# A graph layer on one core: the loop taken in sets of two units, seeds under three parts, and the sixth block of comparisons moved to VectorE

## The chip, the cores and the metric

The kernel runs on one core of a Trainium2 chip. The metric is the device time of one execution in microseconds. Five engines work at once, each through its own queue in order: TensorE (PE; its weight loads are shown as PEld), VectorE (DVE), ScalarE (ACT), GpSimd (POOL) and SyncE (SP), which here only issues DMAs. They wait for each other by semaphores.

## The reference

One layer of a graph network: 6250 nodes of 64 values, 206250 edges sorted by target node.

```python
h = jnp.maximum(_layernorm(x, axis=-1), 0.0)
msg = jax.nn.relu(h[src] + edge_attr)
agg = jax.ops.segment_sum(msg, dst, num_segments=x.shape[0])
out = x + (jax.nn.relu((h + agg) @ W1 + b1) @ W2 + b2)
```

## The kernel before, in words

**Groups and units.** The edges are taken in 269 groups of 768: 128 partitions of G = 6 columns, 64 values each. For most groups the source rows of the first three columns are fetched by GpSimd with three indirect DMAs from a table in DRAM (`gather`, L198, one per column, 128 rows each); the rows of the last three columns (H = 3) are made on the chip by TensorE. Three such columns are a *unit*. In 12 groups (`WHOLE`, L64) all six columns are made on the chip: two units and no gather. After five groups of a prologue, which are gathered entirely, 276 units follow, and two units are a *set*: 138 sets.

**How TensorE fetches rows.** `hp` holds all node rows as three bf16 parts (high, middle, low: 3 x 64 columns), by node. `find` (L446, VectorE) compares the list of wanted nodes with each partition's own number: 0/1 weights `found`. `slots_of` (L478) multiplies them with `hp` and collects the wanted rows into slots; one call makes two of the twelve blocks of a set, here called a *pair of slots*, in a PSUM bank `half` of three. `slots_out` (L486, ScalarE) casts a pair to bf16, `picked`. `back` (L465, VectorE) compares places with `ids` and gives the 0/1 weights `backs` that bring slots back to the edges' order, for five of the six blocks of a set; the sixth is made by two activations on ScalarE (`back_far` L455: a distance; `back_near` L458: relu of one less the distance). `pick` (L493) multiplies `backs` with `picked`, 18 matmuls a unit, into a PSUM buffer `pick` of two banks, of which there are two. It holds four rows of 4 x 64 values: three columns of the unit with their three parts, with the edge attributes as a fourth part (`room`, L499, ScalarE), and in the fourth row the window sums.

**What follows.** `messages` adds the gathered rows to the attributes (L560), reduces the four parts to one sum (L563, VectorE, 768 elements in) and takes the relu (L565, ScalarE). `one_hot` (L544) compares each edge's target with 32 window places; `window_sum` (L575, TensorE) sums the group's messages by target; `sum_into_z` (L538, VectorE) adds the window into `z` at a place held in a register. Every so often a block of 512 nodes is complete, and `hidden`, `result` and `store` write it out. The `rank_*` functions and `source` prepare the lists for three sets at a time, in steps spread over six units (`chunk`); some are matmuls (L277, L315, L329) that wait for VectorE's step before.

**The order.** Scheduling is by hand: each engine works in the order in which the Python code issues. `half(u)` is one unit's turn: window sum of the unit before, three pairs of slots for the set ahead, products of the next unit, z addition of two units before, messages, one-hot, then half of the comparisons. Gathers are issued AHEAD = 9 groups early; their buffers (LOOK = 12) are freed by L560.

Of the kernel before, what the change touches and what calls it, by code (L numbers as in the profile page):

```python
# [81 lines left out]
def kernel(  # L82
# [239 lines left out]
    def source(c):  # L322
# [38 lines left out]
    def ln_turn(r, m, h):  # L361
        zv = z[:D, :NP].rearrange("d (p r) -> d p r", r=RR)
        for i in range(0, m, 4):
            n = min(4, m - i)
            pt = psum.tile([D, 4, PP], F32, name="half", bufs=3)
# [14 lines left out]
    def combine(xg, ea, n):  # L380
        nc.vector.tensor_tensor(xg[:, :n], xg[:, :n], ea[:, :n], ALU.add)
        msg = work.tile([P, G, D], F32, name="msg", bufs=3)
        nc.scalar.activation(msg[:, :n], xg[:, :n], AF.Relu)
        return msg
# [63 lines left out]

    far = const.tile([P, 1], F32, name="far")
    nc.vector.tensor_scalar_mul(far, ids[:, Q - 1:], -1.0)  # L450
    dists = {}

    def back_far(k):
        dists[k] = rank.tile([P, 2 * H * P], BF16, name="dist", bufs=1)
        nc.scalar.activation(dists[k], spots[k].bitcast(I16), AF.Abs, bias=far)  # L455

    def back_near(k):
        nc.scalar.activation(backs[k][:, Q - 1].rearrange("p t s -> p (t s)"), dists.pop(k), AF.Relu,  # L458
                             bias=ones[:, 0:1], scale=-1.0)

    def back(k, q0, q1):
        if q0 == 0:
            backs[k] = hot.tile([P, Q, 2 * H, P], BF16, name="backs")
        for q in range(q0, min(q1, Q - 1)):
            nc.vector.tensor_scalar(backs[k][:, q].rearrange("p t s -> p (t s)"), spots[k].bitcast(I16),  # L465
                                    ids[:, q:q + 1], None, op0=ALU.is_equal)
        if q1 == Q:
            spots.pop(k)

    def slots_of(k, n0):  # L470
        ps = psum.tile([P, 2, 3 * D], F32, name="half", bufs=3)
        for u in range(2):
# [15 lines left out]
    def pick(u0, cols):  # L488
        k, i = divmod(u0, 2)
        ps = picks[u0]  # L490
        for u in cols:
            for q in range(Q):
                nc.tensor.matmul(ps[:, u, :3].rearrange("p t d -> p (t d)"), backs[k][:, q, i * H + u, :],  # L493
                                 picked[k][:, i * Q + q], start=(q == 0), stop=(q == Q - 1))

    def room(u):
        g, c0 = UNITS[u]
        picks[u] = pick_banks[u % 2]
        nc.scalar.copy(picks[u][:, :H, 3], taken[g][0][:, c0:c0 + H])  # L499

# [16 lines left out]
    def norm_edges(xg):  # L517
# [3 lines left out]
        nc.vector.tensor_tensor(xg, xg, s.unsqueeze(2).to_broadcast([P, G, D]), ALU.subtract)  # L521
        sq = work.tile([P, G, D], F32, name="msg", bufs=3)
        nc.scalar.activation(sq, xg, AF.Square)
# [8 lines left out]

    aggs, hots, taken, msgs = {}, {}, {}, {}
    pick_banks = [psum.tile([P, H + 1, 4, D], F32, name=f"pick{i}", bufs=1) for i in range(2)]

    def sum_into_z(u):
# [3 lines left out]
    def one_hot(u):  # L540
        g, (lo, hi) = group_of(u), span(u)
        n = hi - lo
        oh = work.tile([P, G, W], F32, name="oh")
        nc.vector.tensor_tensor(  # L544
# [7 lines left out]

    def messages(u):
        g, (lo, hi) = group_of(u), span(u)
        ea, xg = taken[g]
        m = pool_cols(g)
        if g < RAW:
            norm_edges(xg)
        if m:
            nc.vector.tensor_tensor(ea[:, lo:m], ea[:, lo:m], xg[:, lo:m], ALU.add)  # L560
        if u >= 0:
            c0 = UNITS[u][1]
            nc.vector.tensor_reduce(ea[:, c0:c0 + H], picks.pop(u)[:, :H].rearrange("p j t d -> p j d t"), AX.X, ALU.add)  # L563
        msg = work.tile([P, G, D], F32, name="msg", bufs=3)
        nc.scalar.activation(msg[:, lo:hi], ea[:, lo:hi], AF.Relu)  # L565
        msgs[u] = msg
        if is_last(u):
            taken.pop(g)

    def window_sum(u):  # L570
# [46 lines left out]

    def blocks_behind(u):
        g = group_of(u)
        for c in sorted(res):  # L620
# [3 lines left out]
        for c in range(NB):  # L624
            if READY[c] == g and is_last(u):
                hid[c] = hidden(c)
# [8 lines left out]

    def half(u):
        g = group_of(u)
        k, i = divmod(u, 2)
        first = ((0, 2), (6, 8))[i]
        later = ((4,), (10,))[i]  # L640
        now = is_set(k + 1)
        if is_first(u):
            enter(g + AHEAD)
        if i == 0:
            if is_set(k + 3):
                source_load(k + 3)
        elif is_set(k + 3):
            spot_load(k + 3)
        window_sum(u - 1)
        if u + 1 < U:  # L650
            room(u + 1)
        if now:
            for n0 in first:
                slots_of(k + 1, n0)
                slots_out(k + 1, n0)
            for n0 in later:
                slots_of(k + 1, n0)
        if u + 1 < U:
            pick(u + 1, range(H))
        sum_into_z(u - LAG)  # L660
        blocks_behind(u - LAG)
        messages(u)
        if now:
            for n0 in later:
                slots_out(k + 1, n0)
        one_hot(u)
        if i == 0:
            if is_set(k + 1):
                back_near(k + 1)
                back(k + 1, 3, Q)  # L670
            if is_set(k + 2):
                find(k + 2, 0)
                find(k + 2, BB)
        else:
            if is_set(k + 2):
                back_far(k + 2)
                back(k + 2, 0, 3)
                find(k + 2, 1)
        chunk(u + 14, rank_at)
        chunk(u + 13, rank_count)  # L680
        chunk(u + 12, rank_of)
        chunk(u + 11, rank_marks)
        chunk(u + 11, rank_turn)
        chunk(u + 10, rank_holds)
        chunk(u + 10, rank_fits)
        chunk(u + 9, source)
        if g in CHECKS and is_first(u):
            find_left(CHECKS.index(g))

# [55 lines left out]
    for k in (0, 1):  # L745
        source_load(k)
        spot_load(k)
    for g in range(F0):
        enter(g + AHEAD)
        messages(g - F0)  # L750
        one_hot(g - F0)
# [11 lines left out]
        if g == 3:  # L763
            rank_at(2)
            rank_count(2)
        if g >= 1:
            window_sum(g - 1 - F0)
# [7 lines left out]

    for b in range(BB + 1):
        find(0, b)
    back_far(0)
    back(0, 0, Q)
    back_near(0)  # L780
    for n0 in range(0, 2 * Q, 2):
        slots_of(0, n0)
        slots_out(0, n0)
    source_load(2)
    spot_load(2)
    room(0)
    pick(0, range(H))
    for b in range(BB + 1):
        find(1, b)
    back_far(1)  # L790
    back(1, 0, 3)
    for u in range(U):
        half(u)
    xbs[NB] = old_rows(NB)
    for c in sorted(hid):
        res[c] = result(c, *hid.pop(c))
    window_sum(U - 1)
    for c in sorted(res):
# [19 lines left out]
    with tc.If(any_left > 0):  # L818
        nc.gpsimd.iota(wide, pattern=[[1, WB]], base=1, channel_multiplier=0, allow_small_or_imprecise_dtypes=True)
        with tc.For_i(0, NG, 1) as i:  # L820
# [3 lines left out]
            nc.vector.tensor_copy(lf, left[:, ds(i * G, G)])  # L824
            ea = edge.tile([P, G, D], F32, name="ea")
            nc.sync.dma_start(out=ea.rearrange("p j d -> p (j d)"),
# [3 lines left out]
            all_windows(combine(xa, ea, G), lf, G)  # L830
        ea = edge.tile([P, G, D], F32, name="ea")
        attr_load(ea, NG)
# [45 lines left out]
```

## Time and profile before

| | us |
|---|---|
| runs before (median of 3) | 1771.63 (1760.12 to 1772.58) |
| profiled execution, its own time | 1747.93 |
| its span, first to last instruction | 1746.2 |
| mean granted TensorE clock in it | 0.907 |

Times in the profile are microseconds unless marked ns; a name such as L478 is a line of the kernel. In lists of groups a row has the line, engine, operation, output and input, shapes and count, then busy time, the mean of one in ns, and the engine's idle time just before with what ended it. In a timeline a row has the start, the duration and the instruction, and in brackets the idle time before and its releaser. A matmul's end is modelled, and a busy PE is not PE at its peak. A table by windows gives each engine's busy time in a stretch, with its instructions in parentheses, and the granted clock (PEclk, 1.00 is full).

### The profile page before, as it was taken

Reading aid. Unit: us, or ns where it says so; the run is one execution under the profiler, and the core shown is the slowest. Engines: PE = TensorE matmul, PEld = TensorE weight load, DVE = VectorE, ACT = ScalarE, POOL = GpSimd, SP = SyncE. Lnnn points to the kernel's source line nnn. Section 1 sums busy time; section 2 is a strip of 40 time slices with the busy share of each in tenths; the row PEclk is TensorE's granted clock in tenths of the full one; section 3 lists DMA queues with packets and bytes.
Section 4 is the critical chain, followed back from the end, with each engine's and each line's share of the span. In section 5 each row is a group of like instructions: output and inputs, shape, how many; then the busy total and the mean of one; then the engine's idle time right before and its main releaser. Section 6 shows DMA issues by size and latency. Waiting matters only on the chain.

```text
span 1746.2 us, 54838 instructions
## 1 busy us (share of the span) xinstructions
PE 1302.7 (75%) x23181; PEld 991.3 (57%) x23181; DVE 1024.7 (59%) x2686; ACT 871.5 (50%) x1955; POOL 802.7 (46%) x798
## 2 busy tenths in 40 slices
PE   3047787778778778777777877877777877777787
PEld 2035566556557556565655655655665655565566
DVE  7346556546565665555755655654566566465576
ACT  4235455446455555554544544644554555454465
POOL 6734435444453553544544444444444445444430
PEclk9998889889897898989988988987899889898898
DMA  6223334334333442443433333333333334333341
GB/s 181 66 57 108 103 93 109 91 88 114 99 98 95 114 109 82 108 106 93 117 96 91 106 99 95 104 98 90 94 103 106 93 106 110 86 103 95 97 111 33
DMA packets 115095, 172.34 MB, mean 99 GB/s; under 512 B 28443, under 2 KB 83612, under 8 KB 114844
## 3 DMA queue, kind: packets, MB, share of 16 engines
q1 hardware_dynamic: 89752, 143.03, 27.4%
q0 software_dynamic: 25088, 25.74, 8.3%
q8 instruction: 184, 3.01, 0.7%
q14 instruction: 67, 0.55, 0.1%
q10 hardware_dynamic: 4, 0.01, 0.0%
HBM read 164.85 MB, written 3.84 MB: 97 GB/s over the span
## 4 chain that ended last, share of the span: by engine, by line
PE 64%; issue 18%; another core or an unknown queue 7%; ACT 6%; DVE 3%; POOL 1%; DMA 1%; DVEq 0%; ACTq 0%; POOLq 0%
PE pick L493 28%; PE half L478 24%; PE pick L575 8%; ACT picked L486 2%; PE rows L329 1%; ACT msg L565 1%; PE rows L592 1%; PE rows L603 1%; ACT dist L455 1%; PE rows L279 1%; POOL xg L198 1%; PE rows L277 1%; PE rows L315 0%; ACT backs L458 0%
## 5 line engine op out<-in xcount | busy, mean ns | idle before, releaser
L198 POOL DMA_INDIRECT xg<-h_rows,src_sb x754 | 768.0, 1019 | 865.4 <-DVE ea L560 688.2
L478 PE MATMUL half<-hp,found 128*32 128x192 bf16 x14352 | 500.8, 260 | 215.3 <-issue 191.8
L486 ACT CAST picked<-half 128x384 bf16<-128x384 f32 x828 | 381.1, 477 | 521.7 <-remote 321.7
L493 PE MATMUL pick<-picked,backs 128*128 128x192 bf16 x4968 | 574.6, 267 | 83.9 <-issue 64.2
L493 PEld LDWEIGHTS <-backs 128*128 128x128 bf16 x4968 | 446.6, 106 | 198.1 <-issue 179.6
L478 PEld LDWEIGHTS <-found 128*32 128x32 bf16 x14352 | 340.7, 100 | 320.7 <-issue 284.0
L538 DVE TENSOR_TENSOR z<-z,pick 128x32 f32 x281 | 53.1, 189 | 656.7 <-issue 236.4
L563 DVE TENSOR_REDUCE ea<-pick 128x192 f32<-128x768 f32 x276 | 262.5, 951 | 0.0
L465 DVE TENSOR_SCALAR backs<-spots,ids 128x768 bf16<-128x768 int16 x690 | 251.0, 415 | 0.0
L575 PE MATMUL pick<-oh,msg 128*64 128x32 f32 x3224 | 177.3, 237 | 54.6 <-ACT msg L565 29.5
L446 DVE TENSOR_SCALAR found<-sources,nodes_of 128x1536 bf16<-128x1536 int16 (+1 forms) x414 | 212.4, 542 | 0.1
L575 PEld LDWEIGHTS pick<-oh,msg 128*64 128x64 f32 x3224 | 138.4, 149 | 119.7 <-issue 53.7
L565 ACT ACTIVATE msg<-ea 128x384 f32<-128x384 f32 (+2 forms) x281 | 144.4, 514 | 24.5 <-DVE ea L563 12.8
L499 ACT COPY pick<-ea 128x192 f32<-128x192 f32 x276 | 88.6, 321 | 126.0 <-remote 69.4
L458 ACT ACTIVATE backs<-dist,ones 128x768 bf16<-128x768 bf16 x138 | 130.5, 946 | 0.3 <-ACT dist L455 0.3
L455 ACT ACTIVATE dist<-spots,far 128x768 bf16<-128x768 int16 x138 | 129.9, 941 | 0.0
L544 DVE TENSOR_TENSOR oh<-slot,slots 128x192 f32<-128x192 int16 (+2 forms) x281 | 95.7, 341 | 24.2 <-remote 24.2
L560 DVE TENSOR_TENSOR ea<-ea,xg 128x192 f32<-128x192 f32 x252 | 90.2, 358 | 3.4 <-issue 1.9
L277 PE MATMUL rows<-at,upper 128*128 128x432 f16 x46 | 17.0, 369 | 44.9 <-remote 24.1
L281 ACT CAST before<-rows 128x432 f16<-128x432 f32 x46 | 23.6, 514 | 48.4 <-remote 38.8
L332 ACT CAST source<-rows 24x64 int16<-24x64 f32 x138 | 27.6, 200 | 35.9 <-remote 27.6
L329 PE MATMUL rows<-holds,marks 128*96 128x96 f16 x276 | 27.6, 235 | 15.2 <-DVE oh L544 4.9
(102 smaller groups left out, 435.1 us busy)
## 6 DMA issues: line engine op xcount, KB each, us to landing
sources<-source_row SPq DMA_DIRECT2D x138, 384.0 KB
ea<-in_edge_attr_dram SPq DMA_DIRECT2D x268, 192.0 KB
spots<-spot_rows SPq DMA_DIRECT2D x138, 192.0 KB
xg<-h_rows,src_sb POOLq DMA_INDIRECT x754
xb<-in_x_dram SPq DMA_DIRECT2D x12, 128.0 KB
out_dram<-o SPq DMA_DIRECT2D x12, 128.0 KB
h_rows<-x SPq DMA_DIRECT2D x3, 384.0 KB
dst_sb<-in_dst_main_dram SPq DMA_DIRECT2D x1, 804.0 KB
```

What stands on the lines that cost most here:

```text
L198: nc.gpsimd.indirect_dma_start(out=xg[:, j, :], out_offset=None, in_=rows[:, :], in_offset=bass.IndirectOffsetOnAxis(ap=idx[:, j:j + 1], a ...
L446: nc.vector.tensor_scalar(found[k][:, b * PARTS:b * PARTS + n].rearrange("p m i s -> p (m i s)"), sources[k][:, :n * 2 * S], nodes_of[:, b ...
L455: nc.scalar.activation(dists[k], spots[k].bitcast(I16), AF.Abs, bias=far)
L458: nc.scalar.activation(backs[k][:, Q - 1].rearrange("p t s -> p (t s)"), dists.pop(k), AF.Relu, bias=ones[:, 0:1], scale=-1.0)
L465: nc.vector.tensor_scalar(backs[k][:, q].rearrange("p t s -> p (t s)"), spots[k].bitcast(I16), ids[:, q:q + 1], None, op0=ALU.is_equal)
L478: nc.tensor.matmul(ps[j * S:(j + 1) * S, u], found[k][:, m, i, :], hp[:, min(m, RR - 1)].rearrange("p t d -> p (t d)"), start=(b == 0), st ...
L486: nc.scalar.copy(picked[k][:, n0:n0 + 2], halves.pop((k, n0)))
L493: nc.tensor.matmul(ps[:, u, :3].rearrange("p t d -> p (t d)"), backs[k][:, q, i * H + u, :], picked[k][:, i * Q + q], start=(q == 0), stop ...
L544: nc.vector.tensor_tensor(oh[:, lo:hi], slot[:, g * G + lo:g * G + hi].unsqueeze(2).to_broadcast([P, n, W]), slots.unsqueeze(1).to_broadca ...
L563: nc.vector.tensor_reduce(ea[:, c0:c0 + H], picks.pop(u)[:, :H].rearrange("p j t d -> p j d t"), AX.X, ALU.add)
L565: nc.scalar.activation(msg[:, lo:hi], ea[:, lo:hi], AF.Relu)
L575: nc.tensor.matmul(pa[i * D:(i + 1) * D], msg[:, j, :], oh[:, j, :], start=(j < lo + 2), stop=(j >= hi - 2))
```

## The change

- The loop's turn is a set, `both(k)`, in place of a unit, `half(u)`. Within it the order is: window sums of the two units before; for each of the two units the reduction and addition (`total`), the seeds of the unit two ahead (`room`) and three pairs of slots with their casts; both relus; the products of both units ahead; both z additions; the one-hots; all six blocks of comparisons and three finds for the set two ahead; then the ranking steps of both units.
- `room` seeds the three parts themselves: the attributes under the high part and zeros under the other two. The products are added on top (no `start`), so the reduction takes three parts (576 elements). For one copy to do it, the attribute tiles are twelve buffers of 12 columns, the last six zero, set by ScalarE in the prologue (`tails_begin`); `banks_begin` runs a matmul over each bank of `pick` once.
- In `total` the reduction comes ahead of the addition of gathered rows.
- All six blocks of comparisons are VectorE's; `back_far` and `back_near` are gone.
- The window sums move from the `pick` buffers into the last 128 columns of the three `half` banks, which become named tiles used in turn (`next_half`).
- `msg` and `oh` get four buffers.

```diff
+    eas = [const.tile([P, 2 * G, D], F32, name=f"ea{i}") for i in range(LOOK)]
...
-        ea = edge.tile([P, G, D], F32, name="ea")
-        attr_load(ea, g)
+        ea = eas[g % LOOK]
+        attr_load(ea[:, :G], g)
...
+    half_banks = [psum.tile([P, 512], F32, name=f"half{i}", bufs=1) for i in range(3)]
+    halves_made = [0]
+
+    def next_half():
+        halves_made[0] += 1
+        return half_banks[halves_made[0] % 3]
...
-        for q in range(q0, min(q1, Q - 1)):
+        for q in range(q0, q1):
...
     def slots_of(k, n0):
-        ps = psum.tile([P, 2, 3 * D], F32, name="half", bufs=3)
+        ps = next_half()[:, :2 * 3 * D].rearrange("p (u d) -> p u d", u=2)
...
-                                 picked[k][:, i * Q + q], start=(q == 0), stop=(q == Q - 1))
+                                 picked[k][:, i * Q + q], start=False, stop=(q == Q - 1), skip_group_check=True)
...
-        nc.scalar.copy(picks[u][:, :H, 3], taken[g][0][:, c0:c0 + H])
+        parts = taken[g][0][:, H:].rearrange("p (t c) d -> p c t d", c=H)
+        if c0:
+            nc.scalar.copy(picks[u][:, :H, :3], parts)
+        else:
+            nc.scalar.copy(picks[u][:, :H, 0], taken[g][0][:, :H])
+            nc.scalar.copy(picks[u][:, :H, 1:3], parts[:, :, 1:])
...
+    def banks_begin():
+
+        for t in pick_banks:
+            flat = t.rearrange("p j t d -> p (j t d)")
+            for b in range(0, (H + 1) * 4 * D, 512):
+                nc.tensor.matmul(flat[:, b:b + 512], ones_b, mark_rows[0].rearrange("p g s j -> p (g s j)")[:, :512],
+                                 start=True, stop=True)
+
+    def tails_begin(i):
+        nc.scalar.copy(eas[i][:, G:].rearrange("p j d -> p (j d)"), zero.to_broadcast([P, G * D]))
...
-    def messages(u):
+    def total(u):
         g, (lo, hi) = group_of(u), span(u)
         ea, xg = taken[g]
         m = pool_cols(g)
+        if u >= 0:
+            c0 = UNITS[u][1]
+            nc.vector.tensor_reduce(ea[:, c0:c0 + H], picks.pop(u)[:, :H, :3].rearrange("p j t d -> p j d t"), AX.X, ALU.add)
         if m:
             nc.vector.tensor_tensor(ea[:, lo:m], ea[:, lo:m], xg[:, lo:m], ALU.add)
...
-        pa = pick_banks[u % 2][:, H].rearrange("p t d -> p (t d)")[:, u // 2 % AB * W:][:, :W]
+        pa = half_banks[u % 3][:, 2 * 3 * D + u // 3 % AB * W:][:, :W]
...
+    def both(k):
+        us = (2 * k, 2 * k + 1)
+        ahead = is_set(k + 1)
+        for u in us:
+            if is_first(u):
+                enter(group_of(u) + AHEAD)
+        if is_set(k + 3):
+            source_load(k + 3)
             spot_load(k + 3)
...
+        for u in us:
+            window_sum(u - 2)
+        for u in us:
+            total(u)
+            if ahead:
+                room(u + 2)
+                for n0 in range(u % 2 * Q, u % 2 * Q + Q, 2):
+                    slots_of(k + 1, n0)
+                    slots_out(k + 1, n0)
+        for u in us:
+            relu(u)
+        if ahead:
+            for u in us:
+                pick(u + 2, range(H))
+        for u in us:
+            sum_into_z(u - 2)
+        blocks_behind([u - 2 for u in us])
+        for u in us:
+            one_hot(u)
+        if is_set(k + 2):
+            backs_of(k + 2)
+            for b in range(BB + 1):
+                find(k + 2, b)
+        for u in us:
+            chunk(u + 14, rank_at)
...
+            if group_of(u) in CHECKS and is_first(u):
+                find_left(CHECKS.index(group_of(u)))
```

More of the change, by code (lines that the diff above doesn't have):

```diff
@@ L364, in ln_turn @@
             n = min(4, m - i)
-            pt = psum.tile([D, 4, PP], F32, name="half", bufs=3)
+            pt = next_half()[:D].rearrange("d (u p) -> d u p", u=4)
             for u in range(n):
@@ L381, in combine @@
         nc.vector.tensor_tensor(xg[:, :n], xg[:, :n], ea[:, :n], ALU.add)
-        msg = work.tile([P, G, D], F32, name="msg", bufs=3)
+        msg = work.tile([P, G, D], F32, name="msg", bufs=4)
         nc.scalar.activation(msg[:, :n], xg[:, :n], AF.Relu)
@@ L447, in find @@
                                 sources[k][:, :n * 2 * S], nodes_of[:, b:b + 1], None, op0=ALU.is_equal)
[L449 to L459, printed above, removed]
     def back(k, q0, q1):
@@ L521, in norm_edges @@
         nc.vector.tensor_tensor(xg, xg, s.unsqueeze(2).to_broadcast([P, G, D]), ALU.subtract)
-        sq = work.tile([P, G, D], F32, name="msg", bufs=3)
+        sq = work.tile([P, G, D], F32, name="msg", bufs=4)
         nc.scalar.activation(sq, xg, AF.Square)
@@ L542, in one_hot @@
         n = hi - lo
-        oh = work.tile([P, G, W], F32, name="oh")
+        oh = work.tile([P, G, W], F32, name="oh", bufs=4)
         nc.vector.tensor_tensor(
@@ L556, in messages, with relu @@
         m = pool_cols(g)
-        if g < RAW:
-            norm_edges(xg)
+        if u >= 0:
+            c0 = UNITS[u][1]
+            nc.vector.tensor_reduce(ea[:, c0:c0 + H], picks.pop(u)[:, :H, :3].rearrange("p j t d -> p j d t"), AX.X, ALU.add)
         if m:
             nc.vector.tensor_tensor(ea[:, lo:m], ea[:, lo:m], xg[:, lo:m], ALU.add)
[L561 to L566, printed above, removed]
+        totals[u] = ea
         if is_last(u):
             taken.pop(g)
+    def relu(u):
+        lo, hi = span(u)
+        msg = work.tile([P, G, D], F32, name="msg", bufs=4)
+        nc.scalar.activation(msg[:, lo:hi], totals.pop(u)[:, lo:hi], AF.Relu)
+        msgs[u] = msg
     def window_sum(u):
         (lo, hi), oh, msg = span(u), hots.pop(u), msgs.pop(u)
-        pa = pick_banks[u % 2][:, H].rearrange("p t d -> p (t d)")[:, u // 2 % AB * W:][:, :W]
+        pa = half_banks[u % 3][:, 2 * 3 * D + u // 3 % AB * W:][:, :W]
         for j in range(lo, hi):
@@ L624, in blocks_behind @@
         for c in range(NB):
-            if READY[c] == g and is_last(u):
+            if READY[c] in [group_of(u) for u in us if is_last(u)]:
                 hid[c] = hidden(c)
@@ L634, in is_set @@
         return 0 <= k < KS
[L636 to L647, printed above, removed]
-            spot_load(k + 3)
[L649 to L688, printed above, removed]
@@ new lines, in both @@
+    def both(k):
[6 more added lines that the diff above has]
+            source_load(k + 3)
+            spot_load(k + 3)
+        for u in us:
[23 more added lines that the diff above has]
+            chunk(u + 14, rank_at)
+            chunk(u + 13, rank_count)
+            chunk(u + 12, rank_of)
+            chunk(u + 11, rank_marks)
+            chunk(u + 11, rank_turn)
+            chunk(u + 10, rank_holds)
+            chunk(u + 10, rank_fits)
+            chunk(u + 9, source)
+            if group_of(u) in CHECKS and is_first(u):
+                find_left(CHECKS.index(group_of(u)))
@@ L747 @@
         spot_load(k)
+    banks_begin()
     for g in range(F0):
+        for i in range(g * LOOK // F0, (g + 1) * LOOK // F0):
+            tails_begin(i)
         enter(g + AHEAD)
-        messages(g - F0)
+        if g < RAW:
+            norm_edges(taken[g][1])
+        total(g - F0)
+        relu(g - F0)
         one_hot(g - F0)
@@ L774 @@
     hot = ctx.enter_context(tc.tile_pool(name="hot", bufs=2))
[L776 to L793, printed above, removed]
+    for k in (0, 1):
+        for b in range(BB + 1):
+            find(k, b)
+        backs_of(k)
+        if k == 0:
+            for n0 in range(0, 2 * Q, 2):
+                slots_of(0, n0)
+                slots_out(0, n0)
+            source_load(2)
+            spot_load(2)
+            for u in (0, 1):
+                room(u)
+                pick(u, range(H))
+    for k in range(KS):
+        both(k)
     xbs[NB] = old_rows(NB)
@@ L796 @@
         res[c] = result(c, *hid.pop(c))
+    window_sum(U - 2)
     window_sum(U - 1)
@@ L824 @@
             nc.vector.tensor_copy(lf, left[:, ds(i * G, G)])
-            ea = edge.tile([P, G, D], F32, name="ea")
+            ea = eas[0][:, :G]
             nc.sync.dma_start(out=ea.rearrange("p j d -> p (j d)"),
@@ L830 @@
             all_windows(combine(xa, ea, G), lf, G)
-        ea = edge.tile([P, G, D], F32, name="ea")
+        ea = eas[0][:, :G]
         attr_load(ea, NG)
```

9 lines of the change are left out of this document (5 added, 4 removed).

## The prediction

> **What bounds the kernel now.** I read the busy shares and the chain that ended last, then the waits, and then the instructions in order of time for units with and without gathers.
>
> ```profile
> span 1746.2 us, 54838 instructions
> PE 1302.7 (75%) x23181; PEld 991.3 (57%) x23181; DVE 1024.7 (59%) x2686; ACT 871.5 (50%) x1955; POOL 802.7 (46%) x798
> PE 64%; issue 18%; another core or an unknown queue 7%; ACT 6%; DVE 3%; POOL 1%; DMA 1%; DVEq 0%; ACTq 0%; POOLq 0%
> ...
> POOL xg L198 <- DVE ea L560: 688.2, 220, 19.4
> ACT picked L486 <- remote: 321.7, 147, 6.2
> DVE z L538 <- PE pick L493: 108.9, 33, 7.2
> ```
>
> The chain is TensorE and "issue", a wait for nothing that the profile shows. The wait list says when GpSimd runs: it stands 688.2 us waiting for L560, the addition that frees a gather buffer, so each unit's three gathers start right behind that addition. And ScalarE's cast L486 waits 321.7 us for a releaser that the profile cannot name. Two stretches show what these have to do with each other: one unit with gathers (487.4 on), and one set of two units whose group has none.
>
> ```profile
> core 0: us, PE busy (x) PEld busy (x) DVE busy (x) ACT busy (x) POOL busy (x), PEclk, DMA share, GB/s
> 487.40:492.80 5.40, 3.98 (x86) 3.27 (x82) 3.67 (x11) 2.94 (x8) 2.98 (x3) 1.00 0.54 137
> 682.70:689.60 6.90, 6.84 (x161) 5.92 (x163) 6.39 (x17) 6.56 (x15) 0.00 (x0) 1.00 0.50 176
> ```
>
> At the same clock of 1.00, one unit with gathers takes 5.40 us, and two without take 6.90. The rows say how; first the unit with gathers, then the one without:
>
> ```profile
> 487.43 1.26 PE L478 MATMUL half<-hp,found 128*32 128x192 bf16 x52
> 487.51 0.36 DVE L560 TENSOR_TENSOR ea<-ea,xg 128x192 f32<-128x192 f32 x1
> 488.14 0.94 POOL L198 DMA_INDIRECT xg<-h_rows,src_sb  x1 [1.63 <-DVE ea L560]
> 488.75 0.46 ACT L486 CAST picked<-half 128x384 bf16<-128x384 f32 x1
> 489.39 1.09 POOL L198 DMA_INDIRECT xg<-h_rows,src_sb  x1 [0.30 <-issue]
> 490.26 0.48 ACT L486 CAST picked<-half 128x384 bf16<-128x384 f32 x1 [1.05 <-remote]
> 490.78 0.94 POOL L198 DMA_INDIRECT xg<-h_rows,src_sb  x1 [0.30 <-issue]
> 492.58 0.48 ACT L486 CAST picked<-half 128x384 bf16<-128x384 f32 x1 [1.42 <-remote]
> ...
> 686.43 1.26 PE L478 MATMUL half<-hp,found 128*32 128x192 bf16 x52
> 687.08 0.86 ACT L486 CAST picked<-half 128x384 bf16<-128x384 f32 x2
> ```
>
> The 52 matmuls make three pairs of slots (20, 16, 16). Both times they are through in 1.26 us. Without gathers the first two casts follow at once. With gathers the second comes 2.83 us after the first matmul and the third 5.15, 0.86 after the last gather's end: TensorE's *signals* of finished work come late, one pair in about 2.2 us, until the gathers are over. With five gathers in a row it is worse:
>
> ```profile
> 693.97 0.94 POOL L198 DMA_INDIRECT xg<-h_rows,src_sb  x1 [12.01 <-DVE ea L560]
> ...
> 695.65 0.27 PE L478 MATMUL half<-hp,found 128*32 128x192 bf16 x4
> ...
> 699.81 0.48 ACT L486 CAST picked<-half 128x384 bf16<-128x384 f32 x1 [3.13 <-remote]
> ...
> 701.17 0.94 POOL L198 DMA_INDIRECT xg<-h_rows,src_sb  x1 [0.31 <-issue]
> ...
> 702.75 0.48 ACT L486 CAST picked<-half 128x384 bf16<-128x384 f32 x1 [2.46 <-remote]
> ```
>
> The first cast is 4.2 us behind, the second waits until 0.64 us after the last gather (702.11). Before the change nothing urgent hangs on these casts: VectorE goes on with comparisons and TensorE with products of pairs cast earlier. So gathers, comparisons and casts run side by side.
>
> **The change, part by part.** *ScalarE* loses the two activations that made the sixth block and gets a larger seeding copy. It is busy half the span; the relief is worth nothing unless it sits on the path. *VectorE* makes one more block per set and reads 576 elements per reduction instead of 768; below, both are on the path. TensorE's matmuls stay the same in number.
>
> What decides is order. In the built program the half-bank tiles now hold the pair sums and the window sums together, and the addition into z waits for ScalarE's cast of the fifth or sixth pair of the same set (in one set of three the fourth and fifth), though its window sum was ready long before. Behind that addition VectorE has, in order, both one-hots, the six blocks, the three finds, the ranking work and the next set's first reduction. TensorE's next pairs wait for the finds; the ranking matmuls ahead of them wait for VectorE's ranking work; ScalarE's next seed, with the casts queued behind it, waits for that reduction. It is a ring, and the gathers stand in it: both L560-type additions come right after the reductions at its start, so six gathers run while the six casts are wanted. The row of L538 above shows the same kind of wait already (108.9 us for products in the shared pick banks), but those products were needed at that place anyway.
>
> [...]
>
> Prices for the ring:
>
> ```profile
> L563 DVE TENSOR_REDUCE ea<-pick 128x192 f32<-128x768 f32 x276 | 262.5, 951 | 0.0
> L538 DVE TENSOR_TENSOR z<-z,pick 128x32 f32 x281 | 53.1, 189 | 656.7 <-issue 236.4 <-PE pick L493 108.9 <-ACT msg L565 95.3
> ...
> L288 DVE TENSOR_REDUCE rank_of<-before 128x18 f16<-128x432 f16 x46 | 27.7, 603 | 1.6
> L303 DVE TENSOR_TENSOR holds<-rank_of,from 128x576 f16<-128x576 f16 x46 | 25.3, 551 | 0.0
> L299 DVE TENSOR_TENSOR marks<-at,node 128x432 f16<-128x432 f16 x46 | 20.9, 453 | 0.0
> L272 DVE TENSOR_TENSOR at<-part,from 128x432 f16<-128x432 f16 x46 | 20.8, 451 | 0.0
> ...
> L486 ACT CAST picked<-half 128x384 bf16<-128x384 f32 x828 | 381.1, 477 | 521.7 <-remote 321.7 <-PE half L478 129.4 <-PE rows L315 23.8
> L499 ACT COPY pick<-ea 128x192 f32<-128x192 f32 x276 | 88.6, 321 | 126.0 <-remote 69.4 <-PE pick L575 53.6 <-PE half L478 1.8
> L198 POOL DMA_INDIRECT xg<-h_rows,src_sb x754 | 768.0, 1019 | 865.4 <-DVE ea L560 688.2 <-issue 167.0 <-DVE oh L544 9.5
> ...
> 801.62 0.35 DVE L544 TENSOR_TENSOR oh<-slot,slots 128x192 f32<-128x192 int16 x1
> 801.88 1.07 DVE L465 TENSOR_SCALAR backs<-spots,ids 128x768 bf16<-128x768 int16 x3
> 802.87 0.61 DVE L446 TENSOR_SCALAR found<-sources,nodes_of 128x1536 bf16<-128x1536 int16 x1
> ...
> 809.26 0.95 DVE L446 TENSOR_SCALAR found<-sources,nodes_of 128x1536 bf16<-128x1536 int16 x2
> ```
>
> One set with six gathers, from the end of its first reduction:
> - addition and start of the first gather: 487.51 to 488.14, 0.63 us;
> - six gathers: a start each 1.25 us (488.14 to 489.39), the last 0.94 long: 7.2; at the mean of 1.019 and gaps of 0.30, 7.6. I take 7.2, because VectorE now stands still meanwhile;
> - until TensorE's signals have caught up: 0.86 and 0.64 above; 0.75;
> - what ScalarE still owes: second seed and the last casts. At one pair per 2.2 us only about three pairs are signalled by then; pairs 4 to 6 also wait for casts 1 to 3 to free their banks. Seed and three casts are 1.84 (casts 0.38 apart), three casts 1.24; 1.5. The seed is bounded by one and three of L499 (0.32, 0.96); with the cast's extra 0.156 us per 192 elements it is 0.63;
> - VectorE: second z addition 0.2, two one-hots 0.6, six blocks 2.0 (0.33 apart), three finds 1.5: 4.3;
> - ranking: the four rows are 2.06 us per three sets, 0.7 with small ones left out;
> - reduction: 951 ns times 576/768 is 0.71, with a fixed part 0.75; 0.95 is the bound.
>
> That is 10.1 + 4.3 + 0.7 + 0.75 = 15.8 us. A set without gathers has only the ring: two seeds, six casts and their waits 4.4, then 5.75: 10.1. TensorE's own needs (6.90 for both units without gathers) fit inside.
>
> [...]
>
> The loop runs from the first window sum to the last:
>
> ```profile
> 115.92 0.54 PE L575 MATMUL pick<-oh,msg 128*64 128x32 f32 x12
> ...
> 1737.88 0.64 PE L575 MATMUL pick<-oh,msg 128*64 128x32 f32 x8 [0.78 <-ACT msg L565]
> ```
>
> 1622 us for 138 sets; 124 us lie outside, and the zero copies and bank matmuls of the prologue add 0 to 15, say 10. Twelve groups have no gathers and the last twelve with gathers release none: 36 of 276 units, 18 sets' worth at 6.9 now; so the other 120 sets take (1622 - 124) / 120 = 12.5 us now. After: 120 × 15.8 + 18 × 10.1 + 124 + 10 = 2212 us against 1746.2. The profiled execution took 1747.93, 1.3% under the median shown (1771.63), so I say **2215**. The bounds of the terms together move a set by -0.7 to +1.4 us, the whole to 2128 and 2380.
>
> **The rivals.** *The first three pairs are out before the gathers start* (chance 0.18): TensorE makes them at the tail of the old set. Then pairs 4 to 6 at 2.2 us each end near 8.4 us instead of 10.1, a set takes 14.1, the whole 2008. For it: without gathers three pairs take 1.3 us. Against: TensorE's ranking matmuls and two window sums stand before them, behind VectorE's last work.
>
> *Signals are not late in the new order* (0.10, the other side): six casts follow their matmuls as at 687.08. Then every set is the bare ring of 10.1 us: 134 + 138 × 10.1 = 1528, faster by 13%. It decides if the cast of a pair lags its matmuls by under a microsecond while gathers run; the rows at 490.26, 492.58 and 699.81 speak against it.
>
> *The z wait costs nothing, TensorE under gathers sets the pace* (0.07): 12.5 us as now, near 1746. For it: TensorE's share of the chain. Against: the program's order.
>
> *The change does not do what it says*: it does, the blocks and seeds are in the built program; no chance is kept.
>
> **How the numbers follow.** The forecast has 0.65, the rivals 0.18, 0.10 and 0.07. The range: with these bounds the main case and the first rival span 1924 (2008 less 0.7 us on 120 sets) to 2380; I widen it to 1800 and 2430, for a price of the ring that I missed on either side, and leave out 1528 and most of the third rival. About 1% is what the three runs (1760 to 1773) can tell from no change. Slower: 0.65 + 0.18 + 0.02 of the third rival = 0.85; same 0.03; faster 0.10 + 0.02 = 0.12.
>
> **What would show it.** VectorE's z additions should be its great wait, ended by ScalarE's cast, some 7 us or more in a set; the blocks, finds and ranking should stand behind them with GpSimd idle; GpSimd should run six gathers in a row per set, nearly all of 0.94 us; TensorE's busy share should fall under 65%. Right casts close behind their matmuls during gathers, or finds running while GpSimd gathers, would prove me wrong; so would sets of under 12.5 us.

## The result, and the profile after

| | before | after |
|---|---|---|
| median of the runs, us | 1763.01 (1737.17 to 1772.58) | 2363.66 (2359.51 to 2365.92) |
| ratio, 95% interval | | 1.352 (1.344 to 1.360) |
| profiled execution: its own time, span, clock | 1747.93, 1746.2, 0.907 | 2359.51, 2357.8, 0.767 |

The changed kernel is slower by about 35%; 2215 was forecast, with a range of 1800 to 2430. Some runs of a kernel were up to 3% slower than its fastest; the ratios here and below compare the fast runs only, so they differ a little from the ratios of the medians. The page of after first, its span and busy shares (TensorE had 75%):

```profile
span 2357.8 us, 54280 instructions
...
PE 1495.2 (63%) x23185; PEld 1132.5 (48%) x23185; DVE 998.2 (42%) x2823; ACT 731.3 (31%) x1703; POOL 747.0 (32%) x798
```

Then its groups: busy time and the mean of one, and behind the second bar the idle time before them and what ended most of it.

```profile
L200 POOL DMA_INDIRECT xg<-h_rows,src_sb x754 | 712.8, 945 | 1524.6 <-DVE ea L577 1334.3
...
L486 ACT CAST picked<-half 128x384 bf16<-128x384 f32 x828 | 364.6, 488 | 888.7 <-remote 807.9
L554 DVE TENSOR_TENSOR z<-z,half 128x32 f32 x281 | 53.0, 189 | 1331.5 <-ACT picked L486 1255.7
```

Before, VectorE stood 656.7 us in all in front of the z addition (L538), and the longest part with a name (108.9) was for the products' matmuls; now VectorE stands 1255.7 us in front of it (L554) for ScalarE's cast L486, 9.1 us a set over 138 sets. No engine is busy for more than 63%: a ring of waits, not an engine, sets the time. One set with six gathers, in order of time:

```profile
812.40 0.95 POOL L200 DMA_INDIRECT xg<-h_rows,src_sb  x1 [9.31 <-DVE ea L577]
...
812.68 0.84 PE L478 MATMUL half<-hp,found 128*32 128x192 bf16 x31
...
813.71 0.33 PE L478 MATMUL half<-hp,found 128*32 128x192 bf16 x5 [0.19 <-issue]
...
814.48 0.34 PE L478 MATMUL half<-hp,found 128*32 128x192 bf16 x5 [0.44 <-issue]
...
818.13 0.48 ACT L486 CAST picked<-half 128x384 bf16<-128x384 f32 x1 [5.11 <-remote]
818.65 0.95 POOL L200 DMA_INDIRECT xg<-h_rows,src_sb  x1 [0.30 <-issue]
...
821.00 2.09 PE L478 MATMUL half<-hp,found 128*32 128x192 bf16 x45 [1.08 <-issue]
...
821.09 0.86 ACT L486 CAST picked<-half 128x384 bf16<-128x384 f32 x2 [2.47 <-remote]
...
822.40 1.25 ACT L486 CAST picked<-half 128x384 bf16<-128x384 f32 x3
...
823.69 0.41 DVE L554 TENSOR_TENSOR z<-z,half 128x32 f32 x2 [10.63 <-ACT picked L486]
824.02 0.62 DVE L560 TENSOR_TENSOR oh<-slot,slots 128x192 f32<-128x192 int16 x2
824.56 2.06 DVE L462 TENSOR_SCALAR backs<-spots,ids 128x768 bf16<-128x768 int16 x6
826.53 1.34 DVE L455 TENSOR_SCALAR found<-sources,nodes_of 128x1536 bf16<-128x1536 int16 x3
...
829.30 0.75 DVE L575 TENSOR_REDUCE ea<-pick 128x192 f32<-128x576 f32 x1
```

Read it by who works. From 812.40 to 819.60 GpSimd gathers; TensorE gets through 31 matmuls of the set's 104 and then one to five each 0.75 us or so; the first pair of slots is made by 813.5, and its cast starts at 818.13. At 821.00, 1.4 us after the last gather, the rest of the matmuls come in one piece, and five casts with them. Only then, at 823.69, does VectorE go on: z, one-hots, six blocks, three finds, ranking, and the next reduction at 829.30. From 819.60 to there GpSimd is idle.

### The profile page after: what moved, and what is told of

It reads as the page before. It is cut to its first block, busy times and chain, and to the rows that moved or that the text cites. A ratio compares the mean times of both kernels' runs of the same rounds, so it can differ in the third digit from the quotient of the medians.

```text
span 2357.8 us, 54280 instructions
## 1 busy us (share of the span) xinstructions
PE 1495.2 (63%) x23185; PEld 1132.5 (48%) x23185; DVE 998.2 (42%) x2823; ACT 731.3 (31%) x1703; POOL 747.0 (32%) x798
## 5 line engine op out<-in xcount | busy, mean ns | idle before, releaser
L200 POOL DMA_INDIRECT xg<-h_rows,src_sb x754 | 712.8, 945 | 1524.6 <-DVE ea L577 1334.3
L478 PE MATMUL half<-hp,found 128*32 128x192 bf16 x14352 | 707.1, 299 | 606.2 <-issue 584.4
L478 PEld LDWEIGHTS <-found 128*32 128x32 bf16 x14352 | 427.5, 111 | 843.3 <-issue 827.0
L486 ACT CAST picked<-half 128x384 bf16<-128x384 f32 x828 | 364.6, 488 | 888.7 <-remote 807.9
L554 DVE TENSOR_TENSOR z<-z,half 128x32 f32 x281 | 53.0, 189 | 1331.5 <-ACT picked L486 1255.7
L493 PEld LDWEIGHTS <-backs 128*128 128x128 bf16 x4968 | 529.4, 118 | 70.1 <-issue 51.7
L462 DVE TENSOR_SCALAR backs<-spots,ids 128x768 bf16<-128x768 int16 x828 | 284.3, 413 | 0.0
L575 DVE TENSOR_REDUCE ea<-pick 128x192 f32<-128x576 f32 x276 | 205.6, 749 | 2.5 <-issue 1.7
L501 ACT COPY pick<-ea 128x576 f32<-128x576 f32 x264 | 171.6, 650 | 53.4 <-DVE ea L575 35.2
L593 PE MATMUL half<-oh,msg 128*64 128x32 f32 x3224 | 128.8, 230 | 0.0
L593 PEld LDWEIGHTS half<-oh,msg 128*64 128x64 f32 x3224 | 112.7, 144 | 22.6 <-issue 16.2
```

Of the source, the lines that this page charges most:

```text
L200: nc.gpsimd.indirect_dma_start(out=xg[:, j, :], out_offset=None, in_=rows[:, :], in_offset=bass.IndirectOffsetOnAxis(ap=idx[:, j:j + 1], a ...
L478: nc.tensor.matmul(ps[j * S:(j + 1) * S, u], found[k][:, m, i, :], hp[:, min(m, RR - 1)].rearrange("p t d -> p (t d)"), start=(b == 0), st ...
L486: nc.scalar.copy(picked[k][:, n0:n0 + 2], halves.pop((k, n0)))
L501: nc.scalar.copy(picks[u][:, :H, :3], parts)
L593: nc.tensor.matmul(pa[i * D:(i + 1) * D], msg[:, j, :], oh[:, j, :], start=(j < lo + 2), stop=(j >= hi - 2))
```

## The experiments

The runs fell on chips of two kinds, which matters for reading them. The first result above, and the later job with the changed kernel again, had 1763 and 1733 us for the kernel before; the three other jobs had it at 1105, 1103 and 1104. Below, *late* chips are those of 1733 to 1763 and *prompt* chips those of 1103 to 1105. Each job had one chip at one time, so the runs do not tell what belongs to the chip from what was its state then. Ratios are to the kernel before on the same chip.

**The changed kernel again, on a late chip.** Unchanged.

> The changed kernel itself, on this chip. Two kinds of chip have been seen: one on which the kernel before takes about 1763 us, and one on which it takes about 1105. Theory (the ring through the z addition costs about 10.1 us a set on any chip, and late casts under the gathers come on top on the first kind only): about 1540 to 1580 us where before is near 1105 (ratio about 1.40), and 2360 where before is near 1763. Rival (the ring is only as long as the gathers make the casts late): under 1250 us where before is near 1105.

Measured 2332.29 us (2330.82 to 2335.31), ratio 1.342 (1.332 to 1.353). It repeats the first result. The kernel before beside it took 1738.19 in its profiled execution:

> The kernel before itself, for its trace on this chip. If before is near 1105 us here, both theories expect the casts of the pairs to follow their matmuls by under 1 us while the gathers run, and a unit with gathers to take no longer than one without; if it is near 1763 us, the casts come one pair in about 2.2 us, as shown.

Its page and list of waits are those of the first chip: TensorE 75%, L486 behind "remote" 334.3 us (321.7 there).

**No gathers, in the changed kernel and in the kernel before (prompt chip).** In `load`, the same in both:

```diff
-            xg = edge.tile([P, G - H, D], F32, name="xg")
-        gather(xg[:, lo:], ...)
+            return ea, nothing
```

> The changed kernel without the gathers of the loop: a block of zeros is added in place of the gathered rows, so those messages lack their source rows. Theory (TensorE's signals are late while GpSimd gathers): every set is like the few without gathers now (9.1 us): 134 + 138 x 9.1 = 1390 us, clock higher. Rival (the ring costs the same without gathers, the lateness comes from TensorE's own clock): over 2000 us.

> The kernel before without the gathers of the loop, zeros added in their place. Theory: every set takes the 6.9 us of the sets without gathers: 124 + 138 x 6.9 = 1076 us, so the gathers cost this order some 670 us and the changed one some 970. Rival (gathers only fill idle time): within 10% of 1750 us.

Before without gathers took 1098.67, against 1104.82 with them: on this chip 754 gathers cost next to nothing. By the rows of its reductions (108 and 110 in two stretches of 400 us) that is 7.3 us a set, near the 6.90 that the prediction read from a gather-free set on the late chip. After without gathers took 1547.27, by the rows of its 137 whole sets 10.64 us a set, 5% above the bare ring of 10.1 in the prediction. My expectation for this run (9.1 a set) missed it by more. So the change costs 1.41 without any gather; each of the two kernels was run once.

A part of that length goes with the granted clock, 0.837 in this run and 0.987 in before without gathers. Two windows of this run, each over the 104 matmuls of the six pairs of one set (and a few others that run into it):

```profile
core 0: us, PE busy (x) PEld busy (x) DVE busy (x) ACT busy (x) POOL busy (x), PEclk, DMA share, GB/s
799.70:803.07 3.37, 3.37 (x107) 3.19 (x106) 0.66 (x2) 2.19 (x6) 0.00 (x0) 0.68 0.76 206
820.64:823.10 2.46, 2.46 (x109) 2.21 (x106) 0.39 (x2) 2.16 (x6) 0.00 (x0) 1.00 0.69 150
```

The pairs stand on the ring: in the 18 sets that ran at 1.00 the last cast ends 4.16 us after the first reduction and the set takes 9.27 us, in the 37 at 0.70 to 0.80 it is 5.51 and 11.06 (means). Also at full clock the set is well above 7.3; what the lower clock costs was not tested by itself.

**Gathers in three thirds (prompt chip).** First third: two GpSimd memsets in place of each gather; second: none; last third: the gathers as in the changed kernel.

```diff
+        elif RAW <= g < NG // 3:
+            ...
+                nc.gpsimd.memset(scratch, 0.0)
+                nc.gpsimd.memset(xg[:, j], 0.0)
+            return ea, xg
+        elif g < 2 * NG // 3:
+            return ea, nothing
```

> The changed kernel with its groups in three thirds, to be read by stretches: in the first third each gather is replaced by two GpSimd memsets (about 1 us of GpSimd's time, no DMA), in the second there is no gather, in the last the gathers are as in the changed kernel; the source rows of the gathered columns are left out in the first two. Theory where before is near 1740: last third 16 to 18 us a set, second 10 to 11, and the first tells which part of a gather slows TensorE: near 16 if GpSimd's being busy, 10 to 11 if the DMA. Where before is near 1105: all three thirds 10 to 11 us a set, so that the change costs 1.40 there too; if the last third were 9 us or less, the ring would not be what costs.

The whole took 1549.53, beside 1104.16 for before. A table by windows of the reductions alone (two a set) gives the pace of each third:

```profile
core 0: us, DVE busy (x), PEclk, DMA share, GB/s
100.00:500.00 400.00, 55.92 (x76) 0.83 0.34 95
560.00:960.00 400.00, 55.49 (x75) 0.85 0.33 97
1060.00:1460.00 400.00, 54.85 (x74) 0.85 0.42 114
```

38, 37.5 and 37 sets in 400 us: 10.5, 10.7 and 10.8 us a set. So on a prompt chip the changed kernel's set is the bare ring, gathers or not, and the loss is still 40%, though two thirds of this run have no gathers. One set of the last third, six gathers from 1203.96 to 1211.14:

```profile
1204.79 3.37 PE L489 MATMUL half<-hp,found 128*32 128x192 bf16 x104
...
1205.83 0.48 ACT L497 CAST picked<-half 128x384 bf16<-128x384 f32 x1 [1.24 <-PE half L489]
...
1208.06 1.24 ACT L497 CAST picked<-half 128x384 bf16<-128x384 f32 x3
...
1209.33 0.41 DVE L565 TENSOR_TENSOR z<-z,half 128x32 f32 x2 [4.71 <-ACT picked L497]
```

All 104 matmuls run in 3.37 us under the gathers, the casts right behind them, and z waits 4.71 us, not 10.63. Over the 39 sets of this third with six gathers whose rows are complete, the last cast ends 5.01 us after the end of the first reduction and a set takes 10.76; over the 108 such sets of the first result it is 11.58 and 17.24. The two differences, 6.57 and 6.48, are the same time: on the late chip the gathers delay the casts by it, and the ring passes all of it on.

**GpSimd busy, no DMA (prompt chip).** The memsets in place of all gathers of the loop.

> The changed kernel with each gather replaced by two GpSimd memsets (768 and 64 columns, about 1 us of GpSimd's time) and no DMA; the source rows of the gathered columns are left out. If GpSimd being busy is what makes TensorE slow, this stays above 2200 us where before is near 1740. If the gather's DMA (its descriptors and packets) is what does it, every set is near the bare ring of 10.1 to 11 us: 1530 to 1700. Where before is near 1105 us the run tells nothing of this and should take 1540 to 1700.

1561.39. It fell on a prompt chip, where 1540 to 1700 was expected, and says nothing of the late ones.

**The z additions early (prompt chip).** Only their place in the program changes:

```diff
         for u in us:
             total(u)
+        for u in us:
+            sum_into_z(u - 2)
+        for u in us:
             if ahead:
                 room(u + 2)
...
-        for u in us:
-            sum_into_z(u - 2)
         blocks_behind([u - 2 for u in us])
```

> The changed kernel with one move: both z additions stand right behind the two totals, ahead of the seeds and pairs of the same set, so that they wait for the window sums alone and the comparisons no longer stand behind the casts. Theory (ring through the late casts): VectorE's wait for casts (1255.7 us) goes, comparisons run beside the gathers, and a set of six gathers falls from 17.2 us to the 12 to 13 that gathers, late casts and products need: 1700 to 1850 us. Rival (turn by sets, bigger seeds or the low clock of 0.767 are to blame, the wait only shows it): still over 2200 us.

1180.20 us (1177.35 to 1186.35), ratio 1.068 (1.065 to 1.072); the expectation was for a late chip. The changed kernel itself was not run on a prompt chip; by the runs above, with none or a third of its gathers, it stands at about 1.40 there, so this one move takes back about 370 of 445 us. Its granted clock is 0.944, against 0.836 in the run in thirds, and a part of the gain may be the clock.

```profile
601.88 0.48 DVE L554 TENSOR_TENSOR z<-z,half 128x32 f32 x2
...
602.42 2.52 PE L478 MATMUL half<-hp,found 128*32 128x192 bf16 x104 [0.29 <-DVE z L554]
...
602.82 2.14 DVE L462 TENSOR_SCALAR backs<-spots,ids 128x768 bf16<-128x768 int16 x6
603.13 1.24 ACT L486 CAST picked<-half 128x384 bf16<-128x384 f32 x3 [0.72 <-PE half L478]
```

VectorE makes its blocks while TensorE and ScalarE make the pairs, which is what the ring forbade. A part of the wait has turned round: now the pairs wait for z (the bracket at 602.42; 97.1 us over the span), since they share the bank.

**Window sums in a bank of their own (late chip).** Program order unchanged.

```diff
-    half_banks = [... for i in range(3)]
+    half_banks = [... for i in range(2)]
+    win_bank = psum.tile([P, 512], F32, name="win", bufs=1)
...
-        pa = half_banks[u % 3][...]
+        pa = win_bank[:, u % 16 * W:][:, :W]
```

> The changed kernel with the window sums in a PSUM bank of their own and the pairs in the two half banks that are left; order of the program unchanged. Theory (the z addition waits for the casts only because they share a bank tile): that wait goes, VectorE runs the blocks and finds under the gathers; 1150 to 1250 us where before is near 1105, 1700 to 1950 where it is near 1763. Rival (not the bank, but the work order of a whole set sets the time): within 5% of the changed kernel.

2184.60 us (2181.89 to 2188.67), ratio 1.257 (1.247 to 1.267): 6% below the changed kernel, outside both expectations and nearer to the rival. Its list of waits says where the wait went:

```profile
POOL xg L200 <- DVE ea L578: 1131.0, 130, 16.5
...
ACT picked L487 <- remote: 641.1, 108, 8.4
DVE ea L576 <- PE pick L494: 620.6, 215, 8.0
...
DVE z L555 <- remote: 382.7, 98, 37.5
```

z no longer waits for a cast, and in 77 of the 108 sets with six gathers all six blocks start before the last gather ends. Its wait is not gone: z starts 2.9 us after its window sums' last matmul on the mean, and 382.7 us are put down to a releaser that the profile can't name, as the late casts are. And now the *reduction* waits 620.6 us for the products, which wait for the casts, which come after the gathers. A set with six gathers takes 16.06 us, against 17.04 in the changed kernel beside it. The last cast ends 13.34 us after the end of the first reduction (11.39 there). A part of that is the lack of a third bank for the pairs: TensorE's pairs wait 310.9 us for casts, in the first result 16.2. On a late chip there is thus a second ring, through TensorE's pairs and products, with two banks hardly shorter than the first. How much of the late chip's 35% the wait of z makes by itself isn't shown: the early z additions, which would keep three banks, were not run on such a chip.

**One part alone: six blocks on VectorE (late chip).** The kernel before, without `back_far` and `back_near`:

```diff
-        for q in range(q0, min(q1, Q - 1)):
+        for q in range(q0, q1):
```

> The kernel before with one part of the change alone: the sixth block of comparisons made by VectorE (one more instruction of 0.33 to 0.41 us a set) instead of by two activations on ScalarE. Theory: no ring arises, so the ratio to before is 1.00 to 1.02 on a chip with late casts, and 1.00 to 1.03 where VectorE is near its limit (before near 1105 us). Rival (the added block is itself a large part of the loss): 1.05 or more.

1754.76 us (1730.33 to 1773.73), ratio 1.014 (1.005 to 1.022). The interval does not tell it from no change at the 2% level; the sixth block is at most some 2 of the 35%.

**The loop of before with the change's other parts (prompt chips).** Seeds, blocks and the split addition are kept, `both(k)` gives way to `half(u)`, and three places for the window sums are tried: the half banks as in the change; the pick banks as before; a bank of their own, with two half banks and the third pair behind the products.

```diff
-        pa = half_banks[u % 3][...]                      # first
+        pa = pick_banks[u % 2][:, H]...                  # second
+        pa = win_bank[:, u % 16 * W:][:, :W]             # third
```

> The changed kernel's banks, seeds and six blocks on VectorE, but the turn by units in the order of the kernel before. Theory (a bank shared by pairs and window sums puts the z addition behind a late cast, whatever the turn): a z addition now waits for a cast of its own unit, each unit's comparisons follow its gathers, and a unit takes some 8 to 9 us in place of 6: 2200 to 2500 us. Rival (the turn by sets is what costs): within 5% of 1760 us.

> The changed kernel's seeds, six blocks on VectorE and two-part addition, but with the loop of before (unit by unit) and the window sums in the pick banks as before: no new wait for casts ahead of VectorE's work, no six gathers in a row. Theory (what costs is the order of the set loop and the bank that pairs and window sums share): ratio to before 0.98 to 1.06 on either kind of chip. Rival (the seeds and blocks cost by themselves): 1.10 or more; the same kernel with the window sums in the half banks took 1.149 on the chip where before is near 1105 us, so by the theory the bank alone is most of that 0.149.

> The changed kernel's seeds, six blocks on VectorE and two-part addition, with the loop of before (unit by unit), the window sums in a PSUM bank of their own, the pairs in two half banks, and the third pair of a unit behind the products. Theory (what costs in the change is the loop by sets with its wait and the shared bank, not the seeds and blocks): ratio to before 0.985 to 1.03 on either kind of chip. Rival (a loss of its own in seeds and blocks, or two half banks too few): 1.05 or more.

| window sums in | us | ratio |
|---|---|---|
| half banks, with the pairs | 1269.70 | 1.149 |
| pick banks, as before | 1096.35 (1094.79 to 1099.25) | 0.993 (0.990 to 0.996) |
| a bank of their own | 1153.18 (1149.61 to 1156.10) | 1.045 (1.042 to 1.048) |

(The first was run once; its expectation in us was for a late chip.) In the first the list of waits has the bank's price from both sides, z for the casts and the next window sums for the casts:

```profile
DVE z L554 <- ACT picked L486: 205.7, 176, 3.9
...
PEld half L593 <- ACT picked L486: 106.1, 101, 5.0
```

In the second, casts hold z up for 6.5 us in all and the window sums not at all, and TensorE is busy for 92% of the span, as in before without gathers. It is no version to use: its window sums are opened in the bank in which the products still stand on copied seeds, and its output is off by a relative error of 0.106. That part of the seeded sums is what it leaves out is my reading; how the one disturbs the other is not shown by a run. In the third the longest wait is ScalarE's for the pairs:

```profile
ACT picked L487 <- PE half L479: 219.8, 251, 3.6
```

So seeds and blocks cost nothing that shows on a prompt chip, as far as a kernel with such an output can show it; the shared bank and the order around it do. On a late chip these versions were not run. The third missed both its theory (at most 1.03) and its rival (1.05 or more). Its TensorE stands 16.4 us in all in front of the pairs, 15.8 of it for the finds, so it hardly waits for a cast to free a half bank, and the want of a third bank is not shown; the third pair's place behind the products changed with it, and what makes the 1.045 stays open. No version that computes the whole beat the kernel before.

## Why the prediction was right, and where not

*The ring* is there as described: z is VectorE's great wait, ended by L486, 9.1 us a set (7 or more was named); blocks, finds and ranking stand behind it with GpSimd idle; the gathers take 945 ns on the mean; TensorE is at 63% (under 65% was named). That the ring makes the change a loss without any help from the gathers is shown on the prompt chips: 10.5 to 10.8 us a set against 7.3, in part at a lower clock, and about 1.40 turns into 1.068 when z goes early. On a late chip the waits are those forecast, but no run there took the ring away alone.

*The terms of a set with six gathers*, from the trace's rows, as means over the 108 such sets of the first result:

| term | forecast | measured |
|---|---|---|
| end of the first reduction to the first gather | 0.63 | 0.53 |
| six gathers | 7.2 | 7.19 |
| gathers' end to the last cast's end | 0.75 + 1.5 | 3.85 |
| last cast's end to the last find's end | 4.3 | 4.15, of it 0.14 ahead of the second z addition |
| ranking and reduction | 0.7 + 0.75 | 1.52 |
| set | 15.8 | 17.24 |

The gathers' term took 7.2 and not 7.6 because VectorE stands still meanwhile. In the trace of before the 474 gathers that run beside VectorE's comparisons (L446, L465) take 1059 ns on the mean, the other 280 take 949; in the first result none of the 754 runs beside them, and their mean is 945. Why a gather is longer there is not shown.

The third term was mis-sized by 1.6 us, more than the whole error of the set (1.44). The step that failed is its count of signals: it had three pairs of six signalled when the gathers end, and TensorE caught up 0.75 us later. In the 108 sets 1.3 pairs are cast by then, the next cast starts 1.38 us after the last gather's end, and what is owed takes 2.47 us from there, not 1.5. Behind it stands what the prediction left out: not only TensorE's *signals* are late, its matmuls are held back as well. The first 52 of a set, which make three pairs, take 4.12 us on the mean, against 1.26 in the prediction's unit without gathers and 1.90 under the gathers of the run in thirds, and 61 of 104 are done when the gathers end. The window over the six gathers above has 59 of them and 12 matmuls of the window sums:

```profile
core 0: us, PE busy (x) PEld busy (x) DVE busy (x) ACT busy (x) POOL busy (x), PEclk, DMA share, GB/s
812.40:819.60 7.20, 3.48 (x71) 1.77 (x68) 0.67 (x2) 1.11 (x3) 5.67 (x6) 0.89 0.44 84
```

The trace of before had it already, in the stretch with five gathers in a row:

```profile
696.41 2.23 PE L478 MATMUL half<-hp,found 128*32 128x192 bf16 x41 [0.49 <-issue]
699.00 0.39 PE L478 MATMUL half<-hp,found 128*32 128x192 bf16 x4 [0.36 <-issue]
699.75 0.39 PE L478 MATMUL half<-hp,found 128*32 128x192 bf16 x3 [0.37 <-issue]
```

With the four at 695.65 these are the 52 of a unit: 4.49 us, a part of it at a granted clock of 0.50, with TensorE idle between them. For 120 sets the error of 1.44 us is 173 us more, 2385.

*The mix of sets* gave some of it back. I counted 120 sets with six gathers and 18 with none. In the 136 sets whose rows are complete it is 108 with six, 22 with three at 13.79 us, one with four at 13.78 and 5 with none at 9.08; 108 × 17.24 + 22 × 13.79 + 13.78 + 5 × 9.08 = 2224, and the other 134 (the start, the end and the two last sets) make the 2358 of the span. Single gather-free units were paired with gathering ones, and a mixed set is dearer than the mean of the two kinds by the model, 12.95. The sets without gathers were mis-sized too, 9.08 for a forecast of 10.1, at a granted clock of 1.00 in most of them.

*The first rival* (three pairs out before the gathers) falls: fewer were out, not more. *The third* falls with the set's 17.24 us. *The second* (casts close behind their matmuls, the bare ring of 10.1, 1528 us) falls on the late chips but is what the prompt chips do: 1549.53 with a third of the gathers in place. That the sum came so near is partly luck: the sets were longer than 10.1 and what lies outside them shorter than 134. Even there it is a loss, as the kernel before also gets faster without late casts, to 1104. The prediction held the 1747.93 of its own trace against it and so called it a gain; it did not ask what the same condition does to the kernel before.

*Without the wait the ring's VectorE part (4.3 us) is not simply taken off.* With the wait for casts gone by a bank of its own, and one bank fewer for the pairs, a late chip takes 2184.60, and a set with six gathers is 1 us shorter (16.06 against 17.04): the gathers go on holding TensorE, and the reduction waits 620.6 us for products where z had waited for casts.

## What to carry to other kernels

In a loop ordered by hand, ask of every tile that two uses share which of them the *later reader* will wait for: here a sum ready long before waited for casts of the same bank, and all of VectorE's queue stood behind it; moving the reader ahead of the other use took back most of the loss on a prompt chip. Before a wait is priced at its length, find the next ring: what would be late instead if it were gone. And when a condition is put into a rival ("if signals were not late"), apply it to the kernel before as well.

## What the runs showed of the hardware that I had not expected

Whether gathers hold back TensorE depends on the chip, or on its state at the time. On a late chip the window shown above has 71 matmuls, 59 of the pairs, in 7.20 us of gathers at a clock of 0.89; on a prompt chip the same stretch of the same program (the last third above) has 158, with all 104 of the pairs, at the lower clock of 0.79, so it isn't the clock:

```profile
1203.96:1211.14 7.18, 7.18 (x158) 6.79 (x155) 2.44 (x9) 4.61 (x11) 5.65 (x6) 0.79 0.36 94
```

GpSimd's six gathers take the same time in both (5.67 and 5.65 us busy), so it isn't the gather that is longer, and ScalarE's cast takes 488 ns in the first result and 487 in that run, so ScalarE is not slower either. The kernel before shows it whole: 1733 to 1763 us on the one kind and 1103 to 1105 on the other, the latter within 1% of its time without gathers. What differs between the chips, and whether on the late ones it is GpSimd's work or the gathers' DMA that holds TensorE, stays open: the kernels made for it ran on prompt chips.
